# Summing scan states in pairs by an accumulating GpSimd DMA before TensorE transposes them

## The chip, the cores and the metric

The kernel runs on one core of one Trainium2 chip. The metric is the device time of one execution, in microseconds. Smaller is better.

## What is computed

The input is 16 sequences of 256 tokens with 128 features. A Mamba block with residuals and layer norms comes first, then a feed-forward layer, and then a dense mixture of 8 experts, all of them applied to all tokens. The part that the change touches is the scan of the Mamba block: for each of 256 inner channels and each of 16 states per channel, a recurrence over time, whose products with `C` are summed over the 16 states.

```python
def step(h, inp):
    dA_t, dBx_t, C_t = inp
    h = dA_t * h + dBx_t
    y = jnp.einsum('bdn,bn->bd', h, C_t)      # the sum over n, 16 states
    return (h, y)
...
y = ys.transpose(1, 0, 2)
y = y + D * xc
y = y * jax.nn.silu(z)
return y @ out_proj_w.T
```

The experts are, for each of 8: `h = silu(x @ wg) * (x @ wu)`, `acc = acc + h @ wd`, with 512 hidden features each.

## The kernel before, in words

The 4096 tokens are cut into 8 groups of 512 tokens (two sequences each). Inner channels lie on the partitions, in two halves of 128, tokens on the free dimension. One step of the main loop (lines 567 to 625) handles one state of one half of one group: 32 steps a group, 256 in all. In the same step it handles one slice of the experts (one expert's 128 of 512 hidden features) of an earlier group: 32 slices a group. The order of instructions on each engine is the order in which the code writes them; there is no scheduler. Beside the two, smaller stages are run as generators, a piece per step: `stage_a` prepares the next group (norm, projection, convolution, `B`, `C`, `dt`), `stage_c` finishes the scan of a group (output projection, norm, feed-forward) and `stage_e` finishes the experts.

A step `t` puts these on the engines, in this order:

- SyncE: every second step `fetch` (line 342) loads the rows of `B` and of `C` for two states, broadcast to 128 partitions, 512 KB each, four steps ahead.
- TensorE: `up` (line 484) makes `pg` and `pu` in PSUM; then the transposes of one state (`add_transposed`, line 367); then `down` (line 513), a product of an earlier slice into `acc`.
- ScalarE: `tanh` of `pg` into `eth`, a copy of `pu` into `us` (both in `up`), and the exponential `dA` of the state two steps ahead (`front`, line 350).
- GpSimd: `hidden` (line 507), which multiplies `v` of the slice before by `us`; then `dBx` of the state two steps ahead (line 356).
- VectorE: the scan of the state (line 362), its product with `C` into a tile `hC` of 128x512 (line 364), and `half_gate` (line 498), which gates the slice and frees the PSUM bank of `pg`.

The sum over states is made in PSUM. `sum_states` (line 379) takes the `hC` of a state two steps after its scan (`LAG_Y`, one step where no experts run) and transposes it in four products with the identity, 128x128 each, which accumulate into one bank `y`. The first state of a half is preceded by the transposes of the skip term `D * xc`. There is one bank `y`; after the 16th state of a half `gate` (line 387) multiplies it on VectorE by the gated `z` into `yz`. Its transposes back (`stage_y`) and the output projection follow. `hC` has four buffers, `yz` two.

Of the kernel before, what the change touches and what calls it, by code (L numbers as in the profile page):

```python
# [8 lines left out]
FP = mybir.dt.float32  # L9
AF = mybir.ActivationFunctionType  # L10
ALU = mybir.AluOpType

P = 128
L = 256
DM = 128
NH = 2
NS = 16
DTR = 8
KC = 4
TB = 512  # L20
# [4 lines left out]
NC = 2  # L25
NK = NH * NS
NJ = NE * NF
AHEAD = 2
LAG_Y = 2
LAG_D = 2  # L30
FETCH = 4
START_A = 11
# [7 lines left out]
def kernel(  # L40
# [25 lines left out]
    nc = tc.nc  # L66
    NG = x.shape[0] // TB
# [6 lines left out]
    scan = ctx.enter_context(tc.tile_pool(name="scan", bufs=3))  # L74
# [4 lines left out]
    def bank(tag, name, bufs=1):  # L79
        return ps.tile([P, TB], FP, tag=tag, bufs=bufs, name=name)  # L80
# [12 lines left out]
    def wide(tag, name, bufs):  # L93
        return act.tile([P, TB], FP, tag=tag, bufs=bufs, name=name)
# [12 lines left out]
    def load_x(g):  # L107
        x_tiles[g] = act.tile([P, NTT, DM], FP, tag="xt", bufs=3, name=f"xt{g}")
        nc.sync.dma_start(out=x_tiles[g], in_=xg[g])
# [49 lines left out]
    def as4(t):  # L159
        return t.rearrange("p (c d) -> p c d", d=DM)  # L160

    def norm_stats(src, name):

        st = small.tile([P, NTT, 6], FP, tag="st", name=f"st_{name}")
        mv = small.tile([P, NTT, 2], FP, tag="mv", name=f"mv_{name}")
        for c in range(NTT):
            nc.vector.bn_stats(st[:, c, :], src[:, c, :])
        for c in range(NTT):
            nc.vector.bn_aggr(mv[:, c, :], st[:, c, :])
        ve = small.tile([P, NTT], FP, tag="ve", name=f"ve_{name}")  # L170
        nc.vector.tensor_scalar(ve, mv[:, :, 1], EPS, None, ALU.add)  # L171
        rs = small.tile([P, NTT], FP, tag="rs", name=f"rs_{name}")
        nc.gpsimd.tensor_tensor(rs, ve, mhalf, ALU.pow)  # L173
        return mv, rs

    def norm_shift(stats, name):
        mv, rs = stats
        nb = small.tile([P, NTT], FP, tag="nb", name=f"nb_{name}")
        nc.vector.scalar_tensor_tensor(nb, mv[:, :, 0], -1.0, rs, ALU.mult, ALU.mult)
        return rs, nb  # L180

    def norm_apply(src, dst, scale):
        rs, nb = scale
        for c in range(NTT):
            nc.scalar.activation(  # L185
                dst[:, c, :], src[:, c, :], AF.Identity, bias=nb[:, c : c + 1], scale=rs[:, c : c + 1]
            )

    def transpose(pt, src):

        for c in range(NTT):
            nc.tensor.transpose(pt[:, bass.ts(c, P)], src[:, c, :], ident)

    state = {}
# [4 lines left out]
    def take(name):  # L199

        while len(held) >= limit[0]:
            yield
            yield
        held.add(name)
        return grab(name)

    def done(name):
        held.remove(name)
        give(name)

    def launch(stage, quick=False):

        next(stage)
        running.append([stage, quick])
# [127 lines left out]
    def fetch(g, k):  # L342
        s = state[g]
        n0 = k % NS
        for what, r0 in (("B", n0), ("C", NS + n0)):
            t = scan.tile([P, NC, TB], FP, tag=what, bufs=3, name=f"{what}{g}_{k}")
            nc.sync.dma_start(out=t, in_=s["bc"][r0 : r0 + NC, :].partition_broadcast(P))
            s[what, k // NC] = t
# [10 lines left out]
    def back(g, k):  # L359
        s = state[g]  # L360
        dA, dBx = s.pop(("front", k))
        nc.vector.tensor_tensor_scan(dA, dA, dBx, 0.0, ALU.mult, ALU.add)  # L362
        hC = scan.tile([P, TB], FP, tag="hC", bufs=4, name=f"hC{g}_{k}")
        nc.vector.tensor_mul(hC, dA, s["C", k // NC][:, k % NC, :])  # L364
        s["hC", k] = hC

    def add_transposed(y, src, first, last):
        for c in range(NTT):
            nc.tensor.matmul(  # L369
                y[:, bass.ts(c, P)], lhsT=src[:, bass.ts(c, P)], rhs=ident, is_transpose=True,  # L370
                start=first and c == 0, stop=last and c == NTT - 1, skip_group_check=True,
            )

    def skip(g, h):
        s = state[g]
        t = s["skip", h] = wide("skip", f"skip{g}_{h}", 1)
        nc.scalar.activation(t, s["xc"][:, h, :], AF.Copy, scale=D_sb[:, h : h + 1])

    def sum_states(g, k):
        s = state[g]  # L380
        h, n = divmod(k, NS)
        if n == 0:
            s["y", h] = bank("y", f"y{g}_{h}")
            add_transposed(s["y", h], s.pop(("skip", h)), True, False)
        add_transposed(s["y", h], s.pop(("hC", k)), False, n == NS - 1)

    def gate(g, h):
        s = state[g]
        yz = s["yz", h] = wide("yz", f"yz{g}_{h}", 2)
        nc.vector.tensor_mul(yz, s.pop(("y", h)), s["zg"][:, h, :])  # L390


    def stage_y(g, h):
        s = state[g]
        yield
        pt = yield from take(f"pyt{g}_{h}")
        transpose(pt, as4(s.pop(("yz", h))))
        yield
        if h == 0:
            s["yt"] = act.tile([P, NH, TB], FP, tag="yt", bufs=1, name=f"yt{g}")  # L400
        nc.scalar.copy(s["yt"][:, h, :], pt)
        done(f"pyt{g}_{h}")
        yield
# [117 lines left out]

    def stage_e(g):
        s = state[g]
        ao = wide("ao", f"ao{g}", 1)
        nc.scalar.mul(ao, s["acc"], 0.5)
        yield
        pt = yield from take(f"pao{g}")
        transpose(pt, as4(ao))
        yield
        yield  # L530
        x2 = s["x2"]
        nc.vector.tensor_add(x2, as4(pt), x2)
        done(f"pao{g}")
        stats = norm_stats(x2, f"e{g}")
        yield
        yield
        scale = norm_shift(stats, f"e{g}")
        yield
        norm_apply(x2, x2, scale)
        nc.scalar.dma_start(out=og[g], in_=x2)  # L540
        yield


    scans = [(g, k) for g in range(NG) for k in range(NK)]
# [16 lines left out]
    t = 0  # L561
    j = 0
    queued = 0
    summed = 0
    multiplied = 0
    added = 0
    while added < NG * NJ or running:
        in_scan = t < len(scans)
        in_experts = j < len(slices)
        limit[0] = 1 if in_experts else 2  # L570
        if in_scan:
            g, k = scans[t]
            if k == 0 and 0 < g and g + 1 < NG:
                load_x(g + 1)
            if k == (START_A if g > 0 else 1) and g + 1 < NG:
                running.append([stage_a(g + 1), False])
            t2 = t + FETCH
            if t2 < len(scans) and t2 % NC == 0:
                if "bc" not in state.get(scans[t2][0], {}):
                    raise ValueError("B and C are fetched before they are made")  # L580
                fetch(*scans[t2])
        half()
        if in_experts:
            up(*slices[j])
        half(quick=True)
        half(quick=True)
        lag = LAG_Y if in_experts else 1
        while summed <= min(t - lag, len(scans) - 1):
            gs, ks = scans[summed]
            if ks % NS == 0 and summed:  # L590
                gb, kb = scans[summed - 1]
                gate(gb, kb // NS)
                launch(stage_y(gb, 0) if kb // NS == 0 else stage_c(gb), kb // NS == 1)
            sum_states(gs, ks)
            summed += 1
            if summed == len(scans):
                gate(gs, 1)
                launch(stage_c(gs), True)
        if j > multiplied:
            hidden(*slices[multiplied])  # L600
            multiplied += 1
        if in_scan:
            back(g, k)
            t2 = t + AHEAD
            if t2 < len(scans):
                front(*scans[t2])
                if t2 + 1 < len(scans) and scans[t2 + 1][1] % NS == 0:
                    skip(scans[t2 + 1][0], scans[t2 + 1][1] // NS)
        if in_experts:
            half_gate(*slices[j])  # L610
            j += 1
        if added < (multiplied - 1 if in_experts else multiplied):
            gd, jd = slices[added]
            down(gd, jd)
            added += 1
            if jd == NJ - 1:
                launch(stage_e(gd))
        half()
        if not in_experts:
            half(quick=True)  # L620
            half(quick=True)
        if queued < NG and "x2T" in state.get(queued, {}):
            slices += [(queued, n) for n in range(NJ)]
            queued += 1
        t += 1
# [44 lines left out]
```

## Time and profile before

| | us |
|---|---|
| median of 3 runs (1095.71 to 1100.99) | 1095.85 |
| the profiled execution | 1096.13 |
| its span | 1094.3 |

| group of instructions | count | mean, ns | busy, us |
|---|---|---|---|
| TensorE `y` from `hC` (L369) | 1024 | 291 | 168.1 |
| TensorE `pg` (L488), `pu` (L490), `acc` (L518) | 512 each | 601, 597, 594 | 265.8, 263.8, 262.1 |
| VectorE scan (L362) | 256 | 1223 | 313.1 |
| VectorE product with `C` (L364) | 256 | 692 | 177.1 |
| VectorE `half_gate` (L503) | 256 | 683 | 174.9 |
| GpSimd `v` (L510) | 256 | 1270 | 324.8 |
| GpSimd `dBx` (L356) | 256 | 1272 | 325.1 |

PE is TensorE's matrix products, DVE VectorE, ACT ScalarE, POOL GpSimd, SP SyncE; a `q` behind the name is the engine's queue of instructions. Products of 32-bit numbers appear in two passes, so one `pg` counts twice. PE's products overlap one another in the profile: four transposes in a row take 0.60 us by their own row, and the chain of waits, which gives each instruction only the time until the next one, has 0.44 for them. A chain is the work that ended last, followed back from the end; "issue" in it is time in which an engine waited for nothing that the profile shows. Releasers (`<-`) are what ended an engine's idle time.

### The profile page before, as it was taken

How to read it: one execution, taken by the hardware profiler on the slowest of the kernel's cores; microseconds unless marked ns; L12 is line 12 of the kernel's file. 1: busy time of each engine (PE TensorE's matmuls, PEld its weight loads, DVE VectorE, ACT ScalarE, POOL GpSimd, SP SyncE). 2: the span in 40 equal slices, each digit the busy share in tenths (PEclk: the TensorE clock that was granted, in tenths of full speed). 3: DMA queues.
4: the chain of work that ended last, by engine and by line, in shares of the span. 5: the costliest groups of instructions: out<-in, count | busy, mean ns of one | idle time of the engine just before them, and what ended most of it. 6: DMA issues, size and time to landing. Idle time of an engine off the chain costs nothing.

```text
span 1094.3 us, 11408 instructions
## 1 busy us (share of the span) xinstructions
PE 989.5 (90%) x3488; PEld 516.7 (47%) x3488; DVE 786.0 (72%) x1211; ACT 642.0 (59%) x1091; POOL 710.3 (65%) x591
## 2 busy tenths in 40 slices
PE   4356689997999989999999999999999999999996
PEld 2234545454445554455445554455445555544442
DVE  2689489686897779686987789686987678724222
ACT  3453357754667656755767656655667656544543
POOL 0656367675777757676778667676778668644543
PEclk9575789998999999999999999999999999999998
DMA  8857444352444334452444434452454434100000
GB/s 239 300 192 250 147 154 153 130 190 78 164 157 159 132 117 150 136 185 84 157 163 158 133 118 144 144 176 92 152 169 140 144 124 164 58 0 1 10 1 10
DMA packets 56269, 147.03 MB, mean 134 GB/s; under 512 B 7688, under 2 KB 20880, under 8 KB 56208
## 3 DMA queue, kind: packets, MB, share of 16 engines
q1 hardware_dynamic: 51600, 143.69, 39.5%
q10 hardware_dynamic: 4608, 2.62, 0.8%
q8 instruction: 27, 0.44, 0.2%
q14 instruction: 34, 0.28, 0.1%
HBM read 143.67 MB, written 2.62 MB: 134 GB/s over the span
## 4 chain that ended last, share of the span: by engine, by line
PE 46%; DVE 11%; ACT 3%; issue 2%; POOL 1%; ACTq 0%; POOLq 0%
PE pg L488 11%; PE pu L490 11%; PE acc L518 11%; PE y L369 5%; DVE dA L362 3%; PE pff L455 2%; DVE v L503 2%; PE pf L447 2%; DVE hC L364 1%; ACT x L185 1%; PE po L414 1%; PE pv L276 1%; DVE hc L326 1%; ACT x1h L185 1%; PE pd L262 1%
## 5 line engine op out<-in xcount | busy, mean ns | idle before, releaser
L510 POOL TENSOR_TENSOR v<-v,us 128x512 f32<-128x512 f32 x256 | 324.8, 1270 | 156.4 <-ACT us L494 95.5
L356 POOL TENSOR_TENSOR dBx<-B,u 128x512 f32<-128x512 f32 x256 | 325.1, 1272 | 22.9 <-DVE dA L362 12.1
L362 DVE TENSOR_TENSOR_SCAN dA<-dA,dBx 128x512 f32<-128x512 f32 x256 | 313.1, 1223 | 19.9 <-POOL dBx L356 16.8
L503 DVE SCALAR_TENSOR_TENSOR v<-eth,pg 128x512 f32<-128x512 f32 x256 | 174.9, 683 | 184.6 <-ACT eth L492 184.5
L488 PE MATMUL pg<-x2T,wg 128*128 128x512 f32 x512 | 265.8, 601 | 0.0
L490 PE MATMUL pu<-x2T,wu 128*128 128x512 f32 x512 | 263.8, 597 | 1.9 <-ACT us L494 1.9
L518 PE MATMUL acc<-v,wd 128*128 128x512 f32 x512 | 262.1, 594 | 1.5 <-POOL v L510 1.5
L492 ACT ACTIVATE eth<-pg 128x512 f32<-128x512 f32 x256 | 152.2, 595 | 163.5 <-PE pg L488 159.8
L354 ACT ACTIVATE dA<-dt,A 128x512 f32<-128x512 f32 x256 | 177.6, 694 | 103.5 <-DVE hC L364 101.7
L369 PEld LDWEIGHTS y<-ident,hC 128*128 128x128 f32 x1024 | 133.7, 150 | 149.4 <-issue 100.6
L369 PE MATMUL y<-ident,hC 128*128 128x128 f32 x1024 | 168.1, 291 | 36.1 <-DVE hC L364 36.1
L364 DVE TENSOR_TENSOR hC<-dA,C 128x512 f32<-128x512 f32 x256 | 177.1, 692 | 10.8
L494 ACT COPY us<-pu 128x512 f32<-128x512 f32 x256 | 149.8, 585 | 55.7 <-PE pu L490 55.3
L490 PEld LDWEIGHTS pu<-x2T,wu 128*128 128x128 f32 x512 | 97.0, 191 | 127.7 <-issue 108.3
L488 PEld LDWEIGHTS pg<-x2T,wg 128*128 128x128 f32 x512 | 92.5, 193 | 101.0 <-issue 72.8
L518 PEld LDWEIGHTS acc<-v,wd 128*128 128x128 f32 x512 | 80.3, 191 | 22.1 <-issue 17.6
L173 POOL TENSOR_TENSOR rs_c<-ve_c,mhalf 128x4 f32<-128x4 f32 x8 | 8.1, 1017 | 70.4 <-DVE ve_c L171 70.4
L286 POOL TENSOR_TENSOR u<-dt,xc 128x512 f32<-128x512 f32 x16 | 20.3, 1269 | 41.5 <-ACT dt L282 41.5
L326 DVE SCALAR_TENSOR_TENSOR hc<-pi,cw,hc 128x510 f32<-128x510 f32 (+2 forms) x48 | 35.4, 743 | 6.3 <-ACT hc L319 5.6
L462 DVE TENSOR_TENSOR res<-pff,res 128x512 f32<-128x512 f32 x8 | 5.5, 692 | 42.5 <-PE pff L455 42.5
L173 POOL TENSOR_TENSOR rs_b<-ve_b,mhalf 128x4 f32<-128x4 f32 x8 | 8.1, 1007 | 42.1 <-DVE ve_b L171 42.1
L447 PE MATMUL pf<-h,w 128*128 128x512 f32 x64 | 34.5, 627 | 0.9 <-ACT h L441 0.9
(84 smaller groups left out, 655.9 us busy)
## 6 DMA issues: line engine op xcount, KB each, us to landing
B<-bc SPq DMA_DIRECT2D x128, 512.0 KB, 4.8
C<-bc SPq DMA_DIRECT2D x128, 512.0 KB, 3.9
xt<-in_x_dram SPq DMA_DIRECT2D x8, 256.0 KB, 4.5
wg<-in_Wg_dram SPq DMA_DIRECT2D x8, 256.0 KB, 6.0
wu<-in_Wu_dram SPq DMA_DIRECT2D x8, 256.0 KB, 5.9
wd<-in_Wd_dram SPq DMA_DIRECT2D x8, 256.0 KB, 6.1
out_dram<-x ACTq DMA_DIRECT2D x8, 256.0 KB, 4.8
bc<-dbc ACTq DMA_DIRECT2D x8, 64.0 KB, 2.8
```

Of the source, the lines that this page charges most:

```text
L354: nc.scalar.activation(dA, s["dt"][:, h, :], AF.Exp, scale=A_sb[:, h, n : n + 1])
L356: nc.gpsimd.tensor_tensor(dBx, s["B", k // NC][:, k % NC, :], s["u"][:, h, :], ALU.mult)
L362: nc.vector.tensor_tensor_scan(dA, dA, dBx, 0.0, ALU.mult, ALU.add)
L364: nc.vector.tensor_mul(hC, dA, s["C", k // NC][:, k % NC, :])
L369: nc.tensor.matmul(y[:, bass.ts(c, P)], lhsT=src[:, bass.ts(c, P)], rhs=ident, is_transpose=True, start=first and c == 0, stop=last and c ...
L488: nc.tensor.matmul(pg, lhsT=wg[:, e, bass.ts(f, P)], rhs=s["x2T"], start=True, stop=True)
L490: nc.tensor.matmul(pu, lhsT=wu[:, e, bass.ts(f, P)], rhs=s["x2T"], start=True, stop=True)
L492: nc.scalar.activation(th, pg, AF.Tanh, scale=0.5)
L494: nc.scalar.copy(us, pu)
L503: nc.vector.scalar_tensor_tensor(v, th, 1.0, pg, ALU.add, ALU.mult)
L510: nc.gpsimd.tensor_tensor(v, v, us, ALU.mult)
L518: nc.tensor.matmul(s["acc"], lhsT=wd[:, e, f, :], rhs=s.pop(("h", j)), start=(j == 0), stop=(j == NJ - 1))
```

## The change

The first group is left as it was, apart from the shape of its tiles. From the second group on, the products of four consecutive states lie side by side in one tile of 128 x 4 x 512 (`NQ = 4`), of which there are two buffers. One step after the fourth product, GpSimd issues a DMA that adds the third and fourth quarter of the tile to the first and second, in SBUF (`fold`). TensorE then transposes only the first two quarters, in the steps 6 and 7 after the first of the four (`LAG_Q = 3` steps after the fourth). The last four states of a group's second half are not folded and are transposed as before. There are 7 folds in each of 7 groups.

The plan is worked out ahead: `sums` says which states are transposed in which step, `gates` in which step a half is gated, `folds` in which step a DMA is issued. The gate of the first half comes two steps later than before (its step 20 for 18), that of the second half where it was. In a step, the fold is issued after `dBx` of the state two steps ahead. To make room in SBUF, `yz` has one buffer for two, and `ao` of `stage_e` shares the buffer of `tz`.

```diff
+NQ = 4
+LAG_Q = 3
@@ back
-        hC = scan.tile([P, TB], FP, tag="hC", bufs=4, name=f"hC{g}_{k}")
-        nc.vector.tensor_mul(hC, dA, s["C", k // NC][:, k % NC, :])
-        s["hC", k] = hC
+        if k % NQ == 0:
+            s["hC"] = scan.tile([P, NQ, TB], FP, tag="hC", bufs=2, name=f"hC{g}_{k}")
+        nc.vector.tensor_mul(s["hC"][:, k % NQ, :], dA, s["C", k // NC][:, k % NC, :])
+        s["hC", k] = s["hC"]
@@
+    sums = {}
+    gates = {}
+    folds = {}
+    for g in range(NG):
+        for h in range(NH):
+            whole = []
+            for n in range(NS):
+                k, t = h * NS + n, g * NK + h * NS + n
+                if g == 0:
+                    whole.append((t + 1, k))
+                elif h == NH - 1 and n >= NS - NQ:
+                    whole.append((t + LAG_Y, k))
+                elif n % NQ < NQ // 2:
+                    whole.append((t - n % NQ + NQ - 1 + LAG_Q + n % NQ, k))
+                elif n % NQ == NQ - 1:
+                    folds[t + 1] = g, k
+            whole.sort()
+            for i, (t, k) in enumerate(whole):
+                sums.setdefault(t, []).append((g, k, i == 0, i == len(whole) - 1))
+            gates[whole[-1][0] + 1] = g, h
+
+    def fold(g, k):
+        t = state[g]["hC", k]
+        nc.gpsimd.dma_start(out=t[:, : NQ // 2, :], in_=t[:, NQ // 2 :, :], accum_op=ALU.add)
@@ sum_states
-        add_transposed(s["y", h], s.pop(("hC", k)), False, n == NS - 1)
+        add_transposed(s["y", h], s[("hC", k)][:, k % NQ, :], False, last)
@@ gate
-        yz = s["yz", h] = wide("yz", f"yz{g}_{h}", 2)
+        yz = s["yz", h] = wide("yz", f"yz{g}_{h}", 1)
@@ stage_e
-        ao = wide("ao", f"ao{g}", 1)
+        ao = wide("tz", f"ao{g}", 1)
@@ main loop
-        lag = LAG_Y if in_experts else 1
-        while summed <= min(t - lag, len(scans) - 1):
-            ...
+        if t in gates:
+            gb, hb = gates[t]
+            gate(gb, hb)
+            launch(stage_y(gb, 0) if hb == 0 else stage_c(gb), hb == 1)
+        for what in sums.get(t, ()):
+            sum_states(*what)
...
+        if t in folds:
+            fold(*folds[t])
```

More of the change, by code (lines that the diff above doesn't have):

```diff
@@ L377, in skip, with sum_states @@
         nc.scalar.activation(t, s["xc"][:, h, :], AF.Copy, scale=D_sb[:, h : h + 1])
-    def sum_states(g, k):
+    sums = {}
[21 more added lines that the diff above has]
+        nc.gpsimd.dma_start(out=t[:, : NQ // 2, :], in_=t[:, NQ // 2 :, :], accum_op=ALU.add)
+    def sum_states(g, k, first, last):
         s = state[g]
-        h, n = divmod(k, NS)
-        if n == 0:
+        h = k // NS
+        if first:
             s["y", h] = bank("y", f"y{g}_{h}")
             add_transposed(s["y", h], s.pop(("skip", h)), True, False)
-        add_transposed(s["y", h], s.pop(("hC", k)), False, n == NS - 1)
+        add_transposed(s["y", h], s[("hC", k)][:, k % NQ, :], False, last)
     def gate(g, h):
         s = state[g]
-        yz = s["yz", h] = wide("yz", f"yz{g}_{h}", 2)
+        yz = s["yz", h] = wide("yz", f"yz{g}_{h}", 1)
         nc.vector.tensor_mul(yz, s.pop(("y", h)), s["zg"][:, h, :])
@@ L563 @@
     queued = 0
-    summed = 0
     multiplied = 0
@@ L586 @@
         half(quick=True)
-        lag = LAG_Y if in_experts else 1
-        while summed <= min(t - lag, len(scans) - 1):
[L589 to L598, printed above, removed]
+        if t in gates:
[4 more added lines that the diff above has]
+            sum_states(*what)
         if j > multiplied:
```

## The prediction

> **What bounds the kernel now.** I read in this order: the busy shares and the chain of waits on the page, the chain in order of time inside one group, then the rows of PE and POOL there. "Step" is one turn of the scan loop; a group has 32, numbered from 0, and one group takes 122.8 us (scan of its step 0 at 473.7, of the next group's at 596.5). All times below are from that group.
>
> ```profile
> PE 989.5 (90%) x3488; PEld 516.7 (47%) x3488; DVE 786.0 (72%) x1211; ACT 642.0 (59%) x1091; POOL 710.3 (65%) x591
> PE 46%; DVE 11%; ACT 3%; issue 2%; POOL 1%; ACTq 0%; POOLq 0%
> ```
>
> PE looks like the bound, so every transpose removed looks like time won. The chain in order of time says where that holds. Late in the group it is PE back to back:
>
> ```profile
> 588.22 0.86 PE pg L488 x2
> 589.08 0.86 PE pu L490 x2
> 589.94 0.44 PE y L369 x4
> 590.38 0.86 PE acc L518 x2
> ```
>
> A step is three products of 0.86 and the four transposes of one state, 0.44 in the chain. In the middle of the group the chain is VectorE's and PE's transposes are not on it:
>
> ```profile
> 519.04 1.24 DVE dA L362
> 520.27 0.02 issue
> 520.30 0.69 DVE hC L364
> 520.99 0.59 DVE v L503
> ```
>
> So a group has two kinds of stretch: PE leads in steps 18 to 31 and 0 to 7 (548 to 597, and 474 to 510 but for the wait of the output projection, 488 to 494); VectorE leads in steps 8 to 17 (512 to 548). Which data the fold can have, and when it is needed, stands in the rows of POOL and PE:
>
> ```profile
> 555.35 1.26 POOL L356 TENSOR_TENSOR dBx<-B,u 128x512 f32<-128x512 f32 x1
> 580.37 1.27 POOL L286 TENSOR_TENSOR u<-dt,xc 128x512 f32<-128x512 f32 x1 [2.27 <-ACT dt L282]
> 588.18 1.26 POOL L356 TENSOR_TENSOR dBx<-B,u 128x512 f32<-128x512 f32 x1
> ```
>
> ```profile
> 562.36 0.60 PE L369 MATMUL y<-ident,hC 128*128 128x128 f32 x4
> 592.79 0.60 PE L369 MATMUL y<-ident,hC 128*128 128x128 f32 x4
> ```
>
> POOL is in order, and near step 28 it is late by the two `u` products. For the transfer itself the nearest rows are:
>
> ```profile
> q1 hardware_dynamic: 51600, 143.69, 39.5%
> B<-bc SPq DMA_DIRECT2D x128, 512.0 KB, 4.8
> C<-bc SPq DMA_DIRECT2D x128, 512.0 KB, 3.9
> cw<-in_conv_w_dram SPq DMA_DIRECT2D x1, 4.0 KB, 2.5
> ```
>
> The first gives 0.395 x 16 x 1094.3 us for 143.69 MB: 512 KB keep 16 engines busy for 1.58 us. 4 KB take 2.5 us to land, so about 2.5 us of a landing is not data.
>
> **What the Trainium skill says.** "DMA: Bandwidth & Descriptors", section "SWDGE vs HWDGE vs iDMA": an accumulating transfer can only be issued from GpSimd, whose cores write its descriptors in software; its "Specifications" put the first byte at about 1 us against 0.6 for SP's. "Collectives: The Full Stack", section "The bandwidth ceiling: the fold count and why AG ≠ RS ≠ AR": an add in the transfer costs two source reads, so half the rate of a copy. "Perfetto Trace Analysis", section "DMA Instruction — SWDGE (GPSIMD)": what a profile shows of such an instruction ends with its descriptors, not its data. The trace of before has no GpSimd transfer and no accumulate, so it agrees with none and contradicts none; SP's 2.5, 3.9 and 4.8 us are the only measured neighbours.
>
> **The change, part by part.**
>
> *Transposes removed.* Groups 1 to 7 transpose 10 + 8 states instead of 32: 14 x 7 = 98 states, 392 transposes, at 0.44 us per state 43 us if all were on the path. They are not. Per group, by step: in steps 19 to 31 there were 13 states, there will be 10; in steps 0 to 3 there were 5 (one is the skip term), there will be 2; in steps 4 to 7 the one of step 4 lies ahead of a wait, of the other 3 there will be 3 (skip and two). Saved where PE leads: 6 x 0.44 = 2.6 us. Steps 8 to 17 save 6 more, where VectorE leads: nothing.
>
> *The fold: when can it start, when is it due?* It stands in POOL's order after `dBx` of state 4q+6 (the row's end is its start) and its sum is due two steps later, when PE reaches the transposes; the y's that vanish in between bring PE there sooner.
> - q0: from 496.2; due 501.62 (before: 501.62; one y gone, the skip term put ahead): room 5.4.
> - q1: from 516.2; due 519.88, and the gate on VectorE behind it has 0.5 to spare: 4.2.
> - q2: from 528.9; due 533.7, but the eth that follows waits 3 us for ScalarE anyway: 7.8.
> - q3: from 543.5; before, PE waited there for yz and was through at 549.44; that wait goes since the gate moves to step 20. Against before the fold costs L - 5.5, at best -2.2.
> - q4: from 556.6; due 562.36 - 0.87 + 0.44 (skip first) = 561.9: 5.3.
> - q5: from 569.2; due about 578.1: 8.9.
> - q6: from 589.4 (the second row of dBx above ends there); due 592.79 - 0.87 = 591.9: 2.5.
>
> *How long is the fold (L)?* 2.5 (a small transfer's landing) + 0.4 (software descriptors, the skill's 1 against 0.6) + 2 x 1.58 (two reads) = 6.1 us, an estimate. Bounds: the skill's fit for one GpSimd transfer, 2.0 + bytes/436 GB/s, gives 3.2 for 512 KB read once, 4.4 read twice; upward, another 0.9 (B against C: a neighbour in the queue) and descriptors for three streams from 128 rows, whose price no row shows, give 7 to 8. I take 6.1.
>
> *Sum per group at 6.1:* q0 0.7, q1 1.9, q3 0.6, q4 0.8, q6 3.6, others 0: 7.6 of PE waiting against 2.6 saved: +5.0. Everything behind the waiting transposes on PE waits too: `acc`, the next `pg`, and from that eth, the gate and the next scan. Groups 2 to 6: 25. Group 7 has no next group's `u`, so q6 has room (as q4, plus a step's stage work): +1.4. Group 1 starts without experts and at a clock of 0.6 to 0.9: its saved transposes are dearer and its rooms wider; taken as 0, with 5 either way. **Total +26 us.**
>
> *POOL's time.* 49 issues of about 1 us (the skill's first byte; 0.3, SP's issue row, to 2). Behind each stand `v` and `dBx`. `acc` takes `v` two steps later, with some 4 us to spare; the tightest is q6, where POOL has no idle: `dBx` of state 31 would end at 592.9 instead of 591.9, its scan starts at 593.9. Nothing; if descriptors took over 2 us, the excess would be paid there once a group.
>
> *Edits at nothing.* The products are the same instruction, 0.69. Its tile comes free after the transposes of one step before: in step 28 these end at 582.4, the product starts about 586.5. One yz buffer: its readers are over 10 steps old. `ao` in the buffer of tz: last read 10 steps before. The later gate of half 0 frees no one later: the next y begins at step 22. B and C are fetched five steps ahead; 49 x 3.2 us of transfers in 820 us add 19% to engines that are 43% busy.
>
> The profiled execution took 1096.13 us for a span of 1094.3, the median of the runs is 1095.85, so the difference carries over: **1122 us**.
>
> **Rivals.**
> *The fold lands in time.* One mechanism, L under 5: near the skill's 3.2 to 4.4. At 3.8: q3 -1.7, q6 +1.3, less 2.6: -3.0 in five groups, -4.3 in group 7, -5 in group 1: 1072. For: traffic of B and C is mostly over when a fold starts (at q4 C and B were issued at 553.4 and 553.8). Against: q6's room of 2.5 us is less than the landing of any transfer of 64 KB or more on the page (2.8 and up). It is zero at L = 5.1, faster by 0.5% below 4.9.
> *The accumulate is slow* (descriptors for three streams, or adding below copy rate). At 7: five rooms short, +55, 1151; at 8: +90, 1186. Nothing in the trace excludes it.
> *The gain and the waits cancel*, L about 5: 1093. Removed transposes in steps 8 to 17 are worthless either way.
> *It doesn't do what it says:* no; the order of the built program has 49 folds and 392 transposes less, and the waits for the fold stand on the first transposes only.
>
> **How the numbers follow.** Forecast, L from 5.3 to 7: 0.45. Slow accumulate: 0.17. In time: 0.30. Cancel: 0.08. Slower 0.62, same (within 0.5%, about what this kernel's runs can tell) 0.08, faster 0.30. Signs are mixed; the forecast's own range is 1100 to 1151. The range leaves out L under 3.8 and over 7.4: 1072 to 1165.
>
> **What would show it.** The transposes of y x632 for x1024; a releaser "DMA hC" ahead of them, 1 us in q0, q1, q3, q4 and over 3 in q6, 7 or so per group; folds landing in about 6 us; VectorE's and POOL's busy sums unchanged. Wrong if folds land within 5 us, if PE's waiting sits on q6 alone, or if steps 8 to 17 get shorter.

## The result, and the profile after

The changed kernel takes 1138.53 us (median of 4 runs, 1136.66 to 1139.52) against 1097.15 of the kernel before (4 runs beside it, 1095.71 to 1100.99): a ratio of 1.0367 with a 95% interval of [1.0349, 1.0385], slower by 41 us. The forecast was slower by 26. The profiled execution has a span of 1136.1 us for 1094.3, and TensorE's mean granted clock is 0.934 for 0.952.

From the page after: the busy time of the engines, the chain by engine, the queue of the folds, and (groups of instructions, issues of DMAs) the transposes and the fold. The chain's shares add up to 27% of the span here and to 63% before, so the two aren't compared.

```profile
PE 973.6 (86%) x3096; PEld 486.4 (43%) x3096; DVE 787.2 (69%) x1211; ACT 640.7 (56%) x1091; POOL 752.4 (66%) x640
...
q0 software_dynamic: 7056, 25.69, 12.7%
...
PE 18%; DVE 3%; DMA 2%; POOL 2%; ACT 1%; issue 1%; POOLq 0%; ACTq 0%
...
L372 PE MATMUL y<-ident,hC 128*128 128x128 f32 x632 | 108.5, 305 | 80.0 <-DMA hC<-hC 46.6
...
hC<-hC POOLq DMA_DIRECT2D x49, 512.0 KB, 4.9
```

The same row of the page before:

```profile
L369 PE MATMUL y<-ident,hC 128*128 128x128 f32 x1024 | 168.1, 291 | 36.1 <-DVE hC L364 36.1
```

The transposes went as the plan says, 632 for 1024, and PE has 16 us less to do in a span that is 42 us longer. The last number of the `L372` row is what replaced them: PE stood idle 46.6 us ahead of these transposes, waiting for the fold. Before, the transposes waited 36.1 us, all for VectorE, and 33.3 us of waiting for VectorE are still there.

A fold lands 4.9 us after its issue (median; 4.5 to 7.4), where I had estimated 6.1. The places differ: in groups 2 to 6 it was 4.5 to 5.2 us at q1 to q4, but 5.5 to 5.6 at q6 and 6.3 to 6.6 at q0. (q0 to q7 are a group's fours of states in order; q7 is not folded.) At these two a fetch of `C` was issued right behind the fold, in group 5 1.0 us after it at q6 and 0.6 at q0. On the DMA engines a fold takes 0.127 x 16 x 1136.1 / 49 = 47 us spread over 16 engines, 2.94 us of all of them; I had 3.16.

The dearest wait stands once a group, at the fours q6. First POOL, then PE, in order of time, in group 5:

```profile
739.65 0.87 POOL L406 DMA_DIRECT2D hC<-hC  x1
740.26 1.57 POOL L539 TENSOR_TENSOR v<-v,us 128x512 f32<-128x512 f32 x1
```

```profile
741.32 1.02 PE L519 MATMUL pu<-x2T,wu 128*128 128x512 f32 x2
745.29 1.09 PE L372 MATMUL y<-ident,hC 128*128 128x128 f32 x8 [2.95 <-DMA hC<-hC]
```

The fold starts at 739.65; PE is done with `pu` at 742.3 and gets its data at 745.29, 5.6 us after the start. `acc` and everything behind it wait too.

The time that one group takes, from the scan of its step 0 to that of the next group's (group 7: to the last scan of all), against before, in us:

| group | 1 | 2 | 3 | 4 | 5 | 6 | 7 | sum |
|---|---|---|---|---|---|---|---|---|
| predicted | 0 | +5.0 | +5.0 | +5.0 | +5.0 | +5.0 | +1.4 | +26 |
| measured | +8.0 | +8.0 | +7.3 | +3.5 | +3.4 | +5.9 | +4.4 | +40.5 |

Below, "steps 28 to 31: +2.7" means that the four scans from step 28 on take that much longer than in the kernel before, in group 5 where no group is named. In the changed kernel group 5 reads: steps 0 to 3 -0.41, 4 to 7 +0.88, 8 to 11 +0.78, 12 to 23 +0.12, 24 to 27 -0.71, 28 to 31 +2.72.

### The profile page after: what moved, and what is told of

It is laid out like the page before. It is cut to its first block, busy times and chain, and to the rows that moved or that the text cites. A ratio compares the mean times of both kernels' runs of the same rounds, so it can differ in the third digit from the quotient of the medians.

```text
span 1136.1 us, 10706 instructions
## 1 busy us (share of the span) xinstructions
PE 973.6 (86%) x3096; PEld 486.4 (43%) x3096; DVE 787.2 (69%) x1211; ACT 640.7 (56%) x1091; POOL 752.4 (66%) x640
## 3 DMA queue, kind: packets, MB, share of 16 engines
q0 software_dynamic: 7056, 25.69, 12.7%
## 5 line engine op out<-in xcount | busy, mean ns | idle before, releaser
L539 POOL TENSOR_TENSOR v<-v,us 128x512 f32<-128x512 f32 x256 | 344.4, 1346 | 159.0 <-ACT us L523 113.9
L358 POOL TENSOR_TENSOR dBx<-B,u 128x512 f32<-128x512 f32 x256 | 343.7, 1346 | 20.4 <-DVE dA L364 10.2
L517 PE MATMUL pg<-x2T,wg 128*128 128x512 f32 x512 | 271.9, 613 | 7.9 <-ACT us L523 7.3
L547 PE MATMUL acc<-v,wd 128*128 128x512 f32 x512 | 267.8, 606 | 3.1 <-POOL v L539 3.1
L372 PE MATMUL y<-ident,hC 128*128 128x128 f32 x632 | 108.5, 305 | 80.0 <-DMA hC<-hC 46.6
L372 PEld LDWEIGHTS y<-ident,hC 128*128 128x128 f32 x632 | 82.4, 156 | 149.4 <-DMA hC<-hC 67.4
L547 PEld LDWEIGHTS acc<-v,wd 128*128 128x128 f32 x512 | 88.4, 192 | 73.0 <-issue 58.0
L406 POOL DMA_DIRECT2D hC<-hC x49 | 43.3, 883 | 0.0
L478 ACT ACTIVATE r<-pf,fb 128x512 f32<-128x512 f32 x32 | 22.0, 687 | 26.2 <-PE pf L476 26.2
```

Source lines behind the costliest of these rows:

```text
L358: nc.gpsimd.tensor_tensor(dBx, s["B", k // NC][:, k % NC, :], s["u"][:, h, :], ALU.mult)
L372: nc.tensor.matmul(y[:, bass.ts(c, P)], lhsT=src[:, bass.ts(c, P)], rhs=ident, is_transpose=True, start=first and c == 0, stop=last and c ...
L517: nc.tensor.matmul(pg, lhsT=wg[:, e, bass.ts(f, P)], rhs=s["x2T"], start=True, stop=True)
L539: nc.gpsimd.tensor_tensor(v, v, us, ALU.mult)
L547: nc.tensor.matmul(s["acc"], lhsT=wd[:, e, f, :], rhs=s.pop(("h", j)), start=(j == 0), stop=(j == NJ - 1))
```

## The experiments

My theory: the waits of the transposes for the fold make the loss, and they outweigh a gain of 2.6 us a group. Rivals: GpSimd's time for the issues, the folds' traffic, or the edits to the plan and the buffers make it. Later a second theory came up: part of it is TensorE's clock, which falls after a wait. Each run was timed beside the kernel before; its ratio to that, with the interval in brackets, is what is compared between runs.

**The fold without its wait, and no fold.** `e2_fold_other_way` keeps issue, traffic and place, but adds the other way round, into quarters that nobody transposes; `e3_no_fold` issues nothing. In both, two states of each folded four are missing from the sum.

```diff
# e2_fold_other_way
-        nc.gpsimd.dma_start(out=t[:, : NQ // 2, :], in_=t[:, NQ // 2 :, :], accum_op=ALU.add)
+        nc.gpsimd.dma_start(out=t[:, NQ // 2 :, :], in_=t[:, : NQ // 2, :], accum_op=ALU.add)
# e3_no_fold
-        if t in folds:
-            fold(*folds[t])
```

> The fold stays where it is but adds the first two quarters to the last two, so that what PE transposes doesn't depend on it; the sum leaves out two states of each four that are folded. Same issues on GpSimd, same bytes moved. Theory (waiting): 1070 to 1085. Rival 1 (issuing and traffic): about 1135. Rival 2 (the plan): about 1135.

> The folds are left out; the sum leaves out two states of each four that would be folded. Theory (waiting): 1068 to 1083, within 5 us of the fold that nobody waits for. Rival 1 (issuing and traffic): 1070 to 1085 here too, but then the fold that nobody waits for is 50 us slower than this. Rival 2 (the plan): about 1130.

Measured: 1092.96 us (0.9954 [0.9938, 0.9971] of before) and 1091.57 (0.9943 [0.992, 0.9965]). Taking the wait away takes the whole loss away; the issues and the traffic of 49 folds together cost 1.4 us, which these intervals don't resolve. The rivals GpSimd and traffic fall. So does something of mine: a kernel that has the full saving and no wait for a fold is only 0.5% faster than before, 5 or 6 us and not the 18 of 7 x 2.6. In group 5, without a fold, steps 24 to 27 gain 0.71 and steps 0 to 3 gain 0.84, but steps 4 to 7 *lose* 1.62. All in all nothing is left there: of the 8.0 us that groups 1 to 7 gain in this profile, 6.5 are from groups 1 and 7.

**The plan and the buffers alone.** `e4_all_whole` has the tiles of four, one `yz` buffer, `ao` in the buffer of `tz`, and transposes every state as before.

```diff
-                elif h == NH - 1 and n >= NS - NQ:
+                elif True:
```

> Tiles of four states with two buffers, one yz buffer and ao in the buffer of tz as in the changed kernel, but no folds: all states are transposed, two steps after their scan as before. Theory (waiting) and rival 1: as before, 1092 to 1100. Rival 2, as far as it lies in the tiles and buffers: 1110 or more.

Measured: 1096.16 us, 0.9988 [0.9978, 0.9999], and every group as before to 0.7 us. What I had costed at nothing costs nothing.

**An earlier fold.** `e1_fold_early` issues each fold one step sooner.

```diff
-                    folds[t + 1] = g, k
+                    folds[t] = g, k
```

> The fold is issued one step earlier, after the dBx of the step in which its fourth product is made; nothing else moves. Theory (PE's transposes wait for the fold's landing): the fold starts 3 to 4 us sooner, all waits of y on the DMA go (46.6 us in the changed kernel), what is left is the saving of 2.6 us a group: 1070 to 1085 us, faster than before. Rival 1 (GpSimd's issuing and the DMA traffic cost the time): as much issuing and traffic, about 1135. Rival 2 (the new plan itself, tiles of four with two buffers, transposes bunched in two of four steps, costs the time): about 1135.

Measured: 1121.65 us, 1.0224 [1.0194, 1.0254]: 17 us better than the changed kernel, not 54 to 69. The page has the landing, and the timeline of SP's queue and POOL its cause:

```profile
hC<-hC POOLq DMA_DIRECT2D x49, 512.0 KB, 8.9
```

```profile
678.77 0.32 SPq L349 DMA_DIRECT2D C<-bc  x1
...
679.26 0.89 POOL L406 DMA_DIRECT2D hC<-hC  x1
679.34 0.32 SPq L349 DMA_DIRECT2D B<-bc  x1
```

A step earlier is the moment at which `C` and `B` are fetched too: `C` can be loaded once a product with `C` has freed its buffer, and this product is the one that the fold waits for. The three transfers need 1.58 + 1.58 + 2.94 = 6.1 us of all engines, and the fold lands 8.9 us after its issue instead of 4.9. In group 5, q0 and q1 had room enough (steps 4 to 11 at 0); at q6, where `dBx` behind the two `u` still sets the start, the fold lost in flight what it had gained in start: PE got its data 9.2 us after the issue and waited 2.63 us. Steps 28 to 31 lose 3.9 to 4.5 us in each of groups 1 to 6, 24.8 us in all; that is the whole loss, since elsewhere gains and losses nearly cancel (groups 1 to 7 together: +25.0).

**A copy in place of the sum.** `e6_copy` drops the accumulation.

```diff
-        nc.gpsimd.dma_start(out=t[:, : NQ // 2, :], in_=t[:, NQ // 2 :, :], accum_op=ALU.add)
+        nc.gpsimd.dma_start(out=t[:, : NQ // 2, :], in_=t[:, NQ // 2 :, :])
```

> The fold copies instead of adding (the third and fourth product replace the first and second, which are left out of the sum). Same issue on GpSimd, same place, same waits. If the second read of the accumulate is what makes the landing long: the engines' time per fold falls from 2.94 us to about 1.5 and the landing from 4.9 us to about 3.5, the waits of a steady group from 6.5 us to about 1.7 (q6 only), time about 1098. If the landing is issue and descriptors: landing stays at 4.5 or more and the time at 1125 to 1138.

Measured: 1097.03 us, 0.9993 [0.9983, 1.0003]. From its page:

```profile
q0 software_dynamic: 7056, 25.69, 6.4%
...
hC<-hC POOLq DMA_DIRECT2D x49, 512.0 KB, 3.4
```

The page counts the same 25.69 MB but half the time: 0.064 x 1094.0 / 49 = 1.43 us of all engines a fold, for 2.94 with the sum. "Collectives: The Full Stack" of the Trainium skill (section "The bandwidth ceiling: the fold count and why AG ≠ RS ≠ AR") says an add in the transfer halves the rate, and here it does. The landing fell by 1.5 us as well, so both landings are the data plus 2.0: 3.4 = 1.43 + 2.0 and 4.9 = 2.94 + 2.0. I had put 2.9 for the part that isn't data. And 1.5 us off the median landing (at q6 5.5 to 5.6 became 3.3 to 3.8) is worth 41 us of kernel: this much hangs on the rooms, the times from a fold's start to when PE wants its sum.

**Folds only where nobody waited.** `e7_q4_q5` folds the fours q4 and q5 only.

```diff
-                elif h == NH - 1 and n >= NS - NQ:
+                elif h * NS + n not in range(16, 24):
```

> Folds only for the fours q4 and q5 of each group (14 instead of 49), where PE did not wait for the fold; the other states are transposed whole, two steps after their scan. Theory (only waiting costs): no wait for a fold, steps 24 to 27 at -0.7 us per group as without folds, all others as before: 1090 us. Rival (a fold costs by being there, through POOL or the traffic): 1096 or more.

Measured: 1101.07 us, 1.0029 [1.0019, 1.0038]; slower, if by 3 us. In group 5, steps 16 to 23 gain nothing, 24 to 27 gain 0.71 and 28 to 31 give back 0.87 (the states of q6, transposed whole, now share steps 26 and 27 with those of q5). Why steps 16 to 23 gain nothing is the question that my forecast got wrong, as it had PE leading there. PE around step 21, and then ScalarE at the same time, in order of time:

```profile
680.58 0.65 PE L194 MATMUL pyt<-ident,yz 128*128 128x128 f32 x4
682.91 1.12 PE L517 MATMUL pg<-x2T,wg 128*128 128x512 f32 x2 [1.68 <-ACT us L523]
```

```profile
679.96 0.69 ACT L356 ACTIVATE dA<-dt,A 128x512 f32<-128x512 f32 x1 [1.97 <-DVE hC L367]
...
682.28 0.58 ACT L523 COPY us<-pu 128x512 f32<-128x512 f32 x1
```

With its transposes gone PE comes to `pg` at 681.2 and waits 1.68 us for `us`, which stands on ScalarE behind `dA`, which waits for VectorE's product `hC`. In the kernel before, PE was busy without a gap here, and the same `pg` started at 683.37, only 0.5 later (the two kernels are within 0.1 us of each other at the start of step 16): the chain over VectorE and ScalarE stood right behind PE. PE full is not PE alone.

Group 7 alone lost 3.1 us, at q4, which I had called safe. PE, in order of time:

```profile
924.59 0.60 PE L372 MATMUL y<-ident,skip 128*128 128x128 f32 x4
928.41 0.66 PE L372 MATMUL y<-ident,hC 128*128 128x128 f32 x4 [3.22 <-DMA hC<-hC]
928.90 1.45 PE L547 MATMUL acc<-v,wd 128*128 128x512 f32 x2
930.14 1.91 PE L517 MATMUL pg<-x2T,wg 128*128 128x512 f32 x2
```

Two things come together. PE is there 3.6 us after the fold's start, in group 5 6.0; I take it that this is because group 7 has no next group to prepare. And this fold landed after 6.8 us, at q4 of the other groups after 4.6 to 5.2; a fetch of `C` went out 1.8 us behind it. A `pg` then takes 1.91 us instead of 1.02: the granted clock of this stretch is 0.50.

**TensorE's clock.** The same sign stands in the run without folds in steps 4 and 5, where PE waits for `x1h` ahead of `ph`:

```profile
610.26 1.63 PE L194 MATMUL ph<-ident,x1h 128*128 128x128 f32 x4 [1.60 <-ACT x1h L187]
611.68 1.91 PE L517 MATMUL pg<-x2T,wg 128*128 128x512 f32 x2
613.39 1.70 PE L519 MATMUL pu<-x2T,wu 128*128 128x512 f32 x2
```

In the kernel before, PE has the transposes of two states more to do ahead of that wait, the wait is 0.73 us, and the next `pg` takes 1.02. That it is the clock and not the wait shows within the run without folds: in group 3 the wait is the same, the clock stays at 1.00, and steps 4 to 7 lose nothing (0.00), where they lose 1.53 to 1.69 in groups 4 to 7.

```profile
366.67 1.48 PE L194 MATMUL ph<-ident,x1h 128*128 128x128 f32 x4 [1.59 <-ACT x1h L187]
367.98 1.02 PE L517 MATMUL pg<-x2T,wg 128*128 128x512 f32 x2
```

So `e5_no_fold_fill` gives PE eight products that no one needs (shortened: the bank of `y` is opened in step 4, and the real start in step 6 overwrites them):

```diff
+        if in_scan and g > 0 and k in (4, 5):
+            if k == 4:
+                state[g]["y", 0] = bank("y", f"y{g}_0")
+            add_transposed(state[g]["y", 0], state[g]["skip", 0], True, True)
         for what in sums.get(t, ()):
...
-        if t in folds:
-            fold(*folds[t])
```

> No fold (the third and fourth state of each folded four are left out of the sum, as in the run without folds), and in steps 4 and 5 of groups 1 to 7 PE transposes the skip term once more each, into the bank of y, which the real start of y overwrites: 8 more products per group, 0.88 us of PE work, nothing else. Theory (TensorE's clock): without transposes PE idles 1.6 and 2.4 us ahead of ph, and the clock falls to 0.50 after it; with the filler the idle is about 0.75 us as in the kernel before, the clock stays at 1.00, steps 4 to 7 of a steady group go from +1.65 us against the kernel before to about 0, while steps 0 to 3 stay at -0.85 and 24 to 27 at -0.71. About 1.5 us less per group than without the filler: 1084 us. Rival (work is work): 0.88 us more per group, 1097. Rival (the wait for x1h is ScalarE's and the clock does not matter): 1092, as without the filler.

Measured: 1086.82 us, 0.9901 [0.9883, 0.9918], against 0.9943 [0.992, 0.9965] without the filler. More work, less time. PE in group 5:

```profile
608.43 0.60 PE L372 MATMUL y<-ident,skip 128*128 128x128 f32 x4
...
611.05 1.48 PE L194 MATMUL ph<-ident,x1h 128*128 128x128 f32 x4 [1.16 <-ACT x1h L187]
612.37 1.02 PE L518 MATMUL pg<-x2T,wg 128*128 128x512 f32 x2
```

The wait is 1.16, the clock stays at 1.00, and steps 4 to 7 are at +0.44 for +1.62. The 0.44 are the filler's own price, since group 3 without it had 0.00. It didn't help in every group: in group 7 they were at +2.1 all the same, and in group 3 as well. "TensorE: Matmul & The Clock Gate" of the Trainium skill (Part 1, "What's actually happening") gives the clock two states, full and half, has it fall after an idle window of about 3.4 us or more, and says that this window runs freely, so that the point of the change varies. The halves agree (0.50), and like waits came out both ways here, as with such a window; but waits of 1.6 us were enough.

The changed kernel shows both outcomes of one and the same wait. Its stretches around q6 in group 5 and then in group 6 (from, to, length; busy time and instructions of PE, PEld, DVE, ACT, POOL; granted clock; share of the DMA engines; GB/s):

```profile
743.00:745.00 2.00, 0.00 (x0) 0.00 (x0) 2.00 (x3) 0.71 (x2) 2.00 (x3) 1.00 0.91 145
745.00:747.00 2.00, 1.71 (x10) 1.32 (x11) 1.11 (x2) 0.00 (x0) 2.00 (x3) 1.00 1.02 315
...
869.00:871.00 2.00, 0.00 (x0) 0.00 (x0) 1.97 (x4) 0.85 (x2) 2.00 (x3) 0.89 0.96 115
871.00:873.00 2.00, 1.64 (x8) 1.64 (x9) 1.26 (x2) 0.00 (x0) 2.00 (x3) 0.50 0.96 381
```

PE waited 2.95 us in the one and 2.88 in the other. The clock stayed at 1.00 in the first and fell to 0.50 in the second, and steps 28 to 31 lost 2.72 us there and 5.22 here. The other groups follow the same line. In groups 1 to 6 this wait is 2.88 to 2.95 us; in 2, 4 and 5 the clock held and the steps lost 2.71 to 2.72 us, in 1, 3 and 6 it fell to 0.50 right behind the wait and they lost 4.18, 4.39 and 5.22. That is 5.6 us for the clock, at this one place of the profile. With the earlier fold it fell behind this wait in all six groups.

**Filling the waits of the changed kernel.** `e11_zeros` and `e12_zeros_in_waits` put products of a tile of zeros, added into `y`, ahead of the transposes that wait.

```diff
+ZEROS = 0, 8, 8, 8, 8, 0, 24, 0      # e11; e12: 0, 8, 0, 8, 0, 0, 24, 0
...
+        if g > 0 and k % NQ == 0:
+            for i in range(ZEROS[k // NQ]):
+                nc.tensor.matmul(
+                    s["y", h][:, bass.ts(i % NTT, P)], lhsT=zero, rhs=ident, is_transpose=True,
+                    start=False, stop=False, skip_group_check=True,
+                )
         add_transposed(s["y", h], s[("hC", k)][:, k % NQ, :], False, last)
```

> The changed kernel with products of a tile of zeros ahead of the first transposes of a four, accumulated into y (they change nothing in the sum): 8 for q1 to q4, 24 for q6, at 0.11 us each, so that PE works instead of idling while the fold lands. Theory (part of the loss is TensorE's clock after long waits: in groups 1, 2, 3, 6 and 7 the loss was 8.1, 8.0, 7.2, 6.0 and 4.4 us against 3.3 to 3.6 in groups 4 and 5): all groups fall to about +3.5, so 10 to 16 us less: 1122 to 1128. Rival (the clock does not matter, the products are added work): the same 1138 or up to 5 us more.

> The products of zeros only where a steady group waits long enough to hide them: 8 for q1 and q3, 24 for q6. In the run with zeros also for q2 and q4, steps 20 to 27 became 0.87 us longer in each group than in the changed kernel, which is the zeros of q4 as added work, while the stretches with half a clock after a wait (steps 28 to 31 of groups 1, 3 and 6, steps 12 to 15 of groups 1 and 2) became 1.4 to 2.6 us shorter. Theory (both are true, and they nearly cancelled): without the 0.87 us, 6 us less than that run, 1128 to 1133 us, and clearly less than the changed kernel. Rival (the clock's recovery was chance of one profile): 1136 to 1140, as the changed kernel.

Measured: 1136.5 us, 1.0348 [1.0331, 1.0365], and 1134.03, 1.0318 [1.0304, 1.0333], for 1.0367 [1.0349, 1.0385] of the changed kernel. The first misses its expectation and doesn't differ from the changed kernel by more than the intervals. The second is better than it by some 5 us, with 40 products more a group, though a little short of what I expected. PE at q6 of group 6 in the second:

```profile
866.95 2.78 PE L419 MATMUL y<-ident,zero 128*128 128x128 f32 x24
870.02 1.09 PE L375 MATMUL y<-ident,hC 128*128 128x128 f32 x8 [0.28 <-DMA hC<-hC]
870.95 1.02 PE L556 MATMUL acc<-v,wd 128*128 128x512 f32 x2
```

The clock holds, and steps 28 to 31 of groups 1 and 6 lose 2.75 and 2.67 us instead of 4.18 and 5.22; group 3, where the fold took 7.2 us to land and PE still waited 1.98, loses 4.37 as before. But a `pg` of 1.75 to 1.92 us turned up in step 4 of groups 3, 5 and 7 and in step 9 of group 4, where the changed kernel had one in group 7 only. So the clock is part of the loss, at least these 5 us. For a ceiling there is an estimate: from 148 us on and without the end, the clock stands at 0.50 for 44 us in the trace of the changed kernel and for 10 in that of the kernel before, and in 34 us at half the clock PE does 17 us of work less.

**Looking for a version that beats both.** `e8_early_no_q6_fill` folds early, transposes q6 whole and has the filler of steps 4 and 5. `e9_split` makes two folds of 256 KB out of each, the third product onto the first as soon as it is there; `e10_split_fill` is that with the filler.

```diff
# e8_early_no_q6_fill (and the filler)
-                elif h == NH - 1 and n >= NS - NQ:
+                elif h == NH - 1 and n >= NS - 2 * NQ:
-                    folds[t + 1] = g, k
+                    folds[t] = g, k
# e9_split; e10_split_fill (and the filler)
-                elif n % NQ == NQ - 1:
+                else:
                     folds[t + 1] = g, k
...
-        nc.gpsimd.dma_start(out=t[:, : NQ // 2, :], in_=t[:, NQ // 2 :, :], accum_op=ALU.add)
+        i = k % NQ
+        nc.gpsimd.dma_start(out=t[:, i - NQ // 2, :], in_=t[:, i, :], accum_op=ALU.add)
```

> Fold one step earlier, the four q6 transposed whole as well as q7, and the filler transposes in steps 4 and 5; everything is computed. Theory: no wait of more than 0.5 us for a fold remains (q0 to q3 had none with the early fold, q4 and q5 none at all), the clock stays at 1.00 at ph, so -0.8 us in steps 0 to 7 and -0.7 in 24 to 27 of a steady group: 1084 to 1088 us, faster than the kernel before. Rival (the early fold's meeting with B and C costs elsewhere, in scans that wait for B or C): 1096 or more.

> Each fold split in two of 256 KB: the third product is added to the first one step after it is made, the fourth to the second one step later, 98 issues instead of 49; everything is computed. Theory (the landing against the transposes' time is all): half the bytes twice over should land as the copy of 512 KB did, in about 3.4 us, and the first half is issued a step earlier; no wait for a fold remains, and the kernel is at the level without folds, 1090 to 1094 us. Rival (GpSimd's 0.88 us per issue, now 86 us in all, makes v and dBx late where POOL has no idle, steps 26 to 31): steps 28 to 31 at +2 or more per group, 1105 or more.

> The split fold with the filler transposes of the skip term in steps 4 and 5. Theory: as without folds but with the filler, 1086 to 1090 us, faster than the kernel before by 0.7 to 1%; steps 4 to 7 of a steady group at +0.44 us instead of +1.65. Rival (GpSimd's time): 1100 or more.

Measured: 1104.46 us (1.0051 [1.0032, 1.007]), 1110.85 (1.0116 [1.01, 1.0131]) and 1110.37 (1.0116 [1.0097, 1.0136]). All three missed. In the first, the early fold lands after 8.8 us and PE waits 1.3 us for q3 in groups 3 to 6, which moves no scan; groups 3 and 4 gain 0.4 in steps 0 to 7 and 0.7 in steps 24 to 27, but q6 whole costs the 0.87 of the run with q4 and q5. That leaves -0.2 to +0.1 in groups 3, 4 and 6, and groups 1, 2, 5 and 7 lose 0.6 to 1.7. The halves land late for the same reason as the early fold:

```profile
hC<-hC POOLq DMA_DIRECT2D x98, 256.0 KB, 6.2
```

Half the bytes land after 6.2 us, not 3.4: one of the two goes out beside `B` and `C`. PE waits 0.3 to 1.9 us around steps 30 and 31 in all groups but the last, and 2.87 us in group 7. What the 98 issues cost GpSimd (1.0 us each by their rows) isn't told apart from that. No version with folds that computes the whole sum beat the kernel before; the best without any fold, with the filler, leaves 1% to be had.

## Why the prediction was off

The sign and the mechanism held: "Everything behind the waiting transposes on PE waits too". The size did not: +41 for +26. That is inside the forecast's range (1100 to 1151), but partly by luck. A sign that I had set, "Wrong if folds land within 5 us", came true by the median; groups 1 and 7 were put at +1.4 together and lost 12.4. By its steps:

- **The fold's length.** "I take 6.1" for all places: it was 4.9 as the median, 5.6 at q6 and 6.3 at q0. Twice the copy's engine time is right (2.94 for 3.16); the part that isn't data is 2.0 by the medians, not 2.9. My own sum was "zero at L = 5.1", so 4.9 everywhere would have given no loss. With group 5's own landings it gives waits of 0.9 (q0), 0.7 (q1), -0.6 (q3) and 3.1 (q6), less 2.6: +1.4 a group. The loss was more than that, so other terms were off too.
- **The gain.** "Saved where PE leads: 6 x 0.44 = 2.6 us" failed. Without folds, where the clock happened to hold (group 3), steps 0 to 7 and 24 to 27 gain 0.85 + 0.00 + 0.71 = 1.6 us; with the filler, group 5 gains 0.84 - 0.44 + 0.71 = 1.1. The states in steps 18 to 23 count for nothing, since ScalarE and VectorE are as late as PE there (shown at step 21). And where the clock falls at `ph`, not even that is left.
- **The waits in a steady group.** 0.7, 1.9, 0.6, 0.8 and 3.6 us for q0, q1, q3, q4 and q6 were predicted; in PE's rows of group 5 stand 0.66, 1.03, 1.48, none and 2.95, with 0.36 at q2. q6 makes most of the damage, as predicted (steps 28 to 31: +2.72). The q3 wait, 1.48, moves no scan (steps 12 to 15 are at +0.07), since VectorE leads there. Too much wait against too much gain: +5.0 was forecast, +3.5 and +3.4 are what groups 4 and 5 show.
- **One group for all.** For group 1, "its rooms wider; taken as 0, with 5 either way", and +1.4 for group 7 are the terms that were most off: +8.0 and +4.4, 11 of the 14 us that were missing. In group 1 the landing was no longer (4.6 to 5.6 us); PE came early at q2 (2.9 us after the fold's start, in group 5 4.6; it waited 2.12, and steps 12 to 15 took 3.06 more, with the half clock behind the wait), and the clock fell at q6. In group 2 the shorter room shows as well: at q2 PE came 1.7 us after the fold's start, in group 5 4.6. PE in group 2, in order of time:

```profile
301.48 1.11 PE L372 MATMUL y<-ident,hC 128*128 128x128 f32 x4 [3.29 <-DMA hC<-hC]
302.39 1.91 PE L547 MATMUL acc<-v,wd 128*128 128x512 f32 x2
```

- **The clock.** Absent from the forecast. Groups 2, 3 and 6 lost 4.5, 3.8 and 2.5 us more than the 3.5 of groups 4 and 5. In group 6 the clock explains it (the windows above), in group 3 1.7 us of it, behind q6; the rest of group 3 (2.78 us of waiting at q1) and group 2 are longer waits and the half clock after them, mixed as in the rows above, and I haven't taken them apart.
- **What cost nothing.** GpSimd's issues (0.88 us each by their rows; I had about 1), the traffic, the shared buffers and the later gate: confirmed, 1.4 us between the runs with the turned fold and without it, which is within their intervals, and nothing by the run with the plan alone. But GpSimd's busy sum, which I had unchanged, rose from 710 to 752 us, by the issues and by spans that are drawn longer (below).
- **The rivals' sums.** For L of 7 and 8 my own rooms give +53 and +83 with group 1 at 0, not +55 and +90.

Open: what share of the 41 us the clock has, between the 5 us that products of zeros brought back and the estimate of 17, and why PE reaches q2 3 us sooner in group 2 than in group 5.

## What to carry to other kernels

Taking work off an engine that looks full pays only where no other chain is as late; look at what its next instruction would wait for if it came sooner, and at the last and first turns of the loop, not at one in the middle. A transfer put between two engines is priced by its landing against the room of its reader, at each place and beside what else is fetched at that moment: moved earlier, it may just meet other transfers. And on TensorE a wait of 3 us can cost nearly as much again (5.22 us for 2.72 at q6), since the clock after it may be half.

## What the runs showed that I had not expected

- A sum in the transfer took twice the engines' time of a copy (2.94 and 1.43 us for 512 KB), while the page counts its bytes once.
- Beside `B` and `C` the same fold took 8.9 us to land for 4.9, and 256 KB took 6.2.
- Useless products made a kernel faster, by some 5 us in two runs, and not in a third (the zeros at q1 to q4 and q6).
- After a fold, GpSimd's products show spans of 1.52 to 1.57 us instead of 1.27 (the `v` at 740.26 above), though they start 1.23 us apart as ever; that lasts until GpSimd next idles. The mean of `v` rose from 1270 to 1346 ns, and to 1385 in the run with the turned fold, which lost nothing by it.
